# Linear attention with a router gate: the token blocks laid out as part, chunk, tile, token, each at its own offset modulo 128 B

## The chip, the cores and the metric

One core of one Trainium2 chip runs the whole program in one launch. The metric is the device time in microseconds (us) of one execution. TensorE is called PE here, VectorE DVE, ScalarE ACT, GpSimd POOL and SyncE SP; PEld is PE's row for weight loads. A program of one core has one time per execution, and the figure for a kernel is the median of its runs.

## The reference

The input is 2,048 tokens of 512 features, in 4 batches of 512. All is float32. Cut to what matters:

```
xn   = layernorm(x)                              # over the 512 features
qkv  = silu(xn @ w_qkv.T)                        # 16 heads of 128: q, k, v
out  = lightning attention(q, k, v)              # linear attention with a decay per head, a running 128x128 state
out  = norm_w * out / sqrt(mean(out^2) + 1e-6)   # over the 2,048 head features of a token
gate = sigmoid(xn @ w_gate.T)                    # 2,048 per token
s    = (gate * out) @ w_out.T                    # back to 512 features

p    = softmax(xn @ router_w.T + router_b)       # 64 experts
w    = top 8 of p, the rest 0
u    = xn * sum(w) + w @ expert_bias
x    = x + s * silu(u)
```

Four large products carry the work: those with the v, the q and k, the gate and the output weights.

## The kernel before, in words

**Products.** Each large product is done by a scheme of seven sub-products instead of eight (Strassen's, in Winograd's form). Tokens are split by batch into two halves, and features into two halves of 256. The token side gives seven blocks, `B11`, `T2`, `T3`, `T1`, `B21`, `T4`, `B22` (the list `PRODUCTS`); the `T` blocks are sums of `B` blocks. The weight side gives seven partners, `A11`, `S2` and so on.

**Two parts.** Every operand of these products is split into a high part, rounded to the type `fp32r`, and a low part, the rest (`split_hi` on ACT, L110; `split_lo` on DVE or POOL, L113). A sub-product is made of three passes: high by high, high by low, low by high (`PASSES`). With 256 features as two chunks of 128 (`KC = 2`), each of the seven sub-products takes 2 x 3 = 6 matmuls. `unit` (matmul at L516) runs seven sub-products with their sums; `plain_unit` (L546) runs eight without the scheme, for the first two tiles of tokens.

**The blocks.** The seven blocks of a pair of batches (`p` is 0 or 1) cover `NT = 4` tiles of 128 tokens. A block is one place in SBUF, made by `block`:

```
blocks[p, n] = xpool.tile([P, NT, 2, KC, P], F32R, tag=f"x{slot}", name=f"blk_{n}_{p}")
```

that is, per partition: tile, part, chunk, token, 2,048 values or 8 KB. `p = 0` uses four places of pool `xa` (tags `x0` to `x3`) and three of `xb` (`x4` to `x6`); `p = 1` uses three places of a later pool `xc` and then the four of `xa`.

**Stages.** There are three, one after the other, with some overlap.

1. *V units*, from the start to about 180 us. For 16 combinations of tile and group of weights, `v_unit` makes the v columns. The block is here the stationary operand, 128 tokens of one tile, part and chunk; the moving operand is 512 weight columns. Meanwhile the next tile is normalised, transposed on PE, summed (`token_sums`) and split into its blocks (`split_blocks`). The blocks of `p = 1` are made first in the same places, and stored to DRAM tile by tile (`keep_blocks`, 28 DMAs of SP, L319); those of `p = 0` are then made again from the stored transposes.
2. *Head units*, to about 851 us: for each pair of batches 24 units of two heads' gates, or one head's q and k (`gate_unit`, `qk_unit`). Here the weights, of 128 columns, are stationary, and the block moves, all four tiles of one part and chunk, 512 tokens:

```
return w.of[wn][:, wi, bass.ts(c, P)], blocks[p, xn][:, :, xi, c]
```

   Between sub-products the attention of the head before is run: matmuls `sa` (L672), `kt` (L675), `ss` (L695), `o` (L757, L759) in full fp32. At the change from `p = 0` to `p = 1` the blocks of `p = 1` are loaded from DRAM (`load_block`, L211, seven DMAs of 1 MB).
3. *Output product*, to the end. The matmul at L1228 has 256 moving columns: the split output weights `wr` move, and the split attention results `yr` are stationary. `split_wo` puts the weights of sub-products 1 and 2 into the places `x0` to `x3` of `xa`, which the blocks have left; the others lie in other pools.

**Order.** The schedule is written by hand: the lists `after[0]` to `after[6]` of a unit hold what is issued after each sub-product, and each engine runs its queue in program order. SP issues nearly all DMAs.

Of the kernel before, what the change touches and what calls it, by code (L numbers as in the profile page):

```python
# [1 line left out]

# [6 lines left out]
F32 = mybir.dt.float32  # L9
F32R = mybir.dt.float32r  # L10
# [4 lines left out]
P = 128  # L15
NH = 16
# [4 lines left out]
LN_EPS = 1e-05  # L21
RMS_EPS = 1e-06
WARM = 32

# [14 lines left out]
PRODUCTS = (  # L39
    ("A11", "B11", 0, True),  # L40
    ("S2", "T2", 1, True),
    ("S3", "T3", 2, True),
    ("S1", "T1", 3, True),
    ("A12", "B21", 0, False),
    ("A22", "T4", 2, False),
    ("S4", "B22", 3, False),
)
# [13 lines left out]
def kernel(  # L61
# [13 lines left out]
    nc = tc.nc  # L75
# [5 lines left out]
    NT = N // P  # L81
    KC = FC // 2
    VH = NH // 4
    VW = VH * P
# [3 lines left out]
    def pool(stack, name, bufs=1, **kw):  # L88
        return stack.enter_context(tc.tile_pool(name=name, bufs=bufs, **kw))


    def left(stack, name, bufs=1):
        return pool(stack, name, bufs, side="left", reuse_waits="tile")

    def right(stack, name, bufs=1):
        return pool(stack, name, bufs, side="right", reuse_waits="tile")

    const = pool(ctx, "const")
    wk = pool(ctx, "wk", 2)
    small = pool(ctx, "small", 4)  # L100
    dram = pool(ctx, "dram", space=DRAM)
# [7 lines left out]
    def split_hi(hi, src):  # L109
        nc.scalar.copy(hi, src)  # L110

    def split_lo(eng, lo, src, hi):
        eng.tensor_tensor(lo, src, hi.bitcast(F32), ALU.subtract)  # L113
# [7 lines left out]
    ones = const.tile([P, 1], F32, tag="ones", name="ones")  # L121
    mhalf = const.tile([P, NT], F32, tag="mhalf", name="mhalf")
    W = 2 * P
    decay_row = const.tile([NH, W], F32, tag="decay_row", name="decay_row")
    by_row = const.tile([P, 2], F32, tag="rest_of", name="rest_of")
    rest_of, slope_of = by_row[:, 0:1], by_row[0:NH, 1:2]
    kdecay = const.tile([P, NH], F32, tag="kdecay", name="kdecay")
# [12 lines left out]
    scores_d = [dram.tile([P, NT, E], F32, tag=f"sc{b}", name=f"scd_{b}") for b in range(B)]  # L140
    wT_d = [dram.tile([P, NT, P], F32, tag=f"wT{b}", name=f"wTd_{b}") for b in range(B)]
    blocks_d = {
        n: dram.tile([P, NT, 2, KC, P], F32, tag=f"b{n}", name=f"bd_{n}") for _, n, _, _ in PRODUCTS
    }


    NM, NQ, H2 = len(PRODUCTS), NG // 2, F // 2
# [13 lines left out]
    def warm_up(n):  # L161
        ps = ps_o.tile([P, P], F32, tag="o", name="warm")
        for _ in range(n):
            nc.tensor.transpose(ps, ident, ident)
# [34 lines left out]
    xb_stack = ExitStack()  # L199
    XN = [n for _, n, _, _ in PRODUCTS]  # L200
    NX = 4
    xa = pool(ctx, "xa")
    xb = left(xb_stack, "xb")
    blocks = {}

    def block(p, i, xpool, slot):
        n = XN[i]
        blocks[p, n] = xpool.tile([P, NT, 2, KC, P], F32R, tag=f"x{slot}", name=f"blk_{n}_{p}")

    def load_block(p, i):  # L210
        nc.sync.dma_start(out=blocks[p, XN[i]].bitcast(F32), in_=blocks_d[XN[i]])  # L211
# [47 lines left out]
    def transpose(stage, p, j, t, copy=True):  # L259
        b = p * PB + j  # L260
        if j == 0:
            xfs[p, t] = stage.tile([P, PB, FC, P], F32, tag="xf", name=f"xf_{p}_{t}", bufs=2)
        pt = ps_sc.tile([P, FC, P], F32, tag="sc", name=f"pt_{b}_{t}")
        for c in range(FC):
            nc.tensor.transpose(pt[:, c, :], xts[b, t][:, bass.ts(c, P)], ident)
        if copy:
            nc.scalar.copy(xfs[p, t][:, j], pt)
        return pt
# [3 lines left out]

    def split_blocks(p, t, eng, srcs):
        for n, src in srcs:
            blk = blocks[p, n][:, t]
            split_hi(blk[:, 0], src)
            split_lo(eng, blk[:, 1], src, blk[:, 0])


    def token_sums(eng, xf, s):  # L280
# [35 lines left out]

    def keep_blocks(p, t):
        for n in XN:
            nc.sync.dma_start(out=blocks_d[n][:, t], in_=blocks[p, n].bitcast(F32)[:, t])  # L319


    lg = {}
# [214 lines left out]
    def plain_unit(name, operands, sink, after):  # L537
        for i in range(2):
            ps = [ps_mm.tile([P, N], F32, tag="mm", name=f"d{i}{j}_{name}") for j in range(2)]
            for k in range(2):  # L540
                for j in range(2):
                    xn = (("B11", "T1"), ("B21", "B22"))[k][j]
                    for c in range(KC):
                        for n, (wi, xi) in enumerate(PASSES):
                            lhsT, rhs = operands(f"A{i + 1}{k + 1}", xn, wi, xi, c)
                            nc.tensor.matmul(  # L546
                                ps[j], lhsT, rhs, start=(k == 0 and c == 0 and n == 0),
                                stop=(k == 1 and c == KC - 1 and n == len(PASSES) - 1),
                            )
                    if k == 1:  # L550
                        sink(i, j, ps[j])
                for fs in (after[0:1], after[1:3], after[3:5], after[5:7])[2 * i + k]:
                    for f in fs:
                        f()
# [4 lines left out]
    def silu_of(dst, src, then=None):  # L559
        nc.scalar.activation(dst, src, AF.Silu)  # L560
        if then is not None:
            then()


    def v_weights(p, g, rawp, sump, wp):
        def loads(raw):
            r = raw.rearrange("p i k (c w) -> p i k c w", c=KC)
            per = VH // GH
            return [
                (r[:, i, k, :, bass.ts(j, GH * P)], w_v[(2 * g + i) * per + j][:, bass.ts(k, KC)])  # L570
                for i in range(2) for k in range(2) for j in range(per)
            ]
        return Weights(f"v_{p}_{g}", KC * VW, rawp, sump, wp, loads, True)

    def v_unit(p, g, t, w, outp, after, direct=False):
        name = f"v_{p}_{g}_{t}"

        def operands(wn, xn, wi, xi, c):
            return blocks[p, xn][:, t, xi, c], w.of[wn][:, wi, bass.ts(c, VW)]

        def sink(i, j):
            dst = outp.tile([P, VW], F32, tag="vout", name=f"vo{i}{j}_{name}")

            def store():
                nc.sync.dma_start(out=v_d[p * PB + j, 2 * g + i][t], in_=dst)
            return dst, lambda src: silu_of(dst, src, store)

        if direct:
            plain_unit(name, operands, lambda i, j, ps: sink(i, j)[1](ps), after)
            return  # L590
        unit(
            name, operands, lambda ps: sink(0, 0)[1](ps),
            [lambda: sink(1, 1), lambda: sink(0, 1), lambda: sink(1, 0)], after,
        )
# [11 lines left out]

    def head_operands(p, w):
        def operands(wn, xn, wi, xi, c):
            return w.of[wn][:, wi, bass.ts(c, P)], blocks[p, xn][:, :, xi, c]
        return operands  # L610


# [247 lines left out]
    def split_wo(m, j, w):  # L860
        pool_, tag = (
            (op, f"w{m}{j}") if m == 0 else (xa, f"x{2 * m - 2 + j}") if m < 3 else (late, f"w{min(m % 6, m)}{j}")
        )
        if m == 6:
            tag = f"w3{j}"
        wr = pool_.tile([P, 2, NQ, H2], F32R, tag=tag, name=f"wr_{m}_{j}", bufs=1)
        split_hi(wr[:, 0], w)
        for i in range(2):
            c = bass.ts(i, NQ // 2)
            split_lo(nc.vector if m else nc.gpsimd, wr[:, 1, c], w[:, c], wr[:, 0, c])  # L870
        wos[m, j] = wr
# [104 lines left out]
    stage = right(vs_stack, "stage", 4)  # L976
    rawp, sump = right(vs_stack, "vraw"), right(vs_stack, "vsum")
    vwp, vout = left(vw_stack, "vw", 8), left(vw_stack, "vout", 4)
    ws = [v_weights(0, g, rawp, sump, vwp) for g in range(NV)]
    tiles = [(p, t) for p in range(NP) for t in range(NT)]  # L980
    again = [(p, t) for p in reversed(range(NP)) for t in range(NT)]
# [17 lines left out]
    sig = small.tile([P, NT], F32, tag="var", name="table")  # L999
    warm_up(WARM)  # L1000
    for i, n in enumerate(XN):
        block(0, i, xa if i < NX else xb, i)
        blocks[1, n] = blocks[0, n]
# [8 lines left out]
    pt = [transpose(stage, 0, j, 0, False) for j in range(PB)]  # L1012
    nc.vector.tensor_copy(xfs[0, 0][:, 0], pt[0])
    b11, b12, b21, b22 = halves(xfs[0, 0])
    split_hi(blocks[0, "B11"][:, 0, 0], pt[0][:, 0:KC])
    ws[0].split_one("A11", nc.vector, hi=True)
    split_lo(nc.gpsimd, blocks[0, "B11"][:, 0, 1], b11, blocks[0, "B11"][:, 0, 0])
    nc.scalar.copy(xfs[0, 0][:, 1], pt[1])
    nc.sync.dma_start(out=xf_d[0], in_=xfs[0, 0])
    load_pair(stage, *tiles[2])  # L1020
# [11 lines left out]
    for k, (p, t) in enumerate(tiles + again):  # L1032
# [22 lines left out]
        if k < NP_FIRST:  # L1055
            for i in range(2 * k, 2 * k + 2):
                after[2 + 2 * (i % 2)].append(lambda i=i: ws[0].sum_of(i, nc.vector))
            for i, n in enumerate((("S1", "S2"), ("S3", "S4"))[k]):
                eng = nc.gpsimd if i else nc.vector
# [37 lines left out]


    attp = right(ha_stack, "att", 2)
    xc = None  # L1100
    xc_stack = ExitStack()

    steps = [(p, m, g) for p in range(NP) for m in range(NM) for g in range(NG)]
# [30 lines left out]
    for i, (p, kind, n, w) in enumerate(todo):  # L1134
# [102 lines left out]
    for i, (p, m, g) in enumerate(steps):  # L1237
# [111 lines left out]
```

## Time and profile before

| What | Value |
|---|---|
| Median of 3 runs | 1058.5 us (1058.11 to 1059.04) |
| The profiled execution | 1058.03 us |
| Its span, first to last instruction | 1056.2 us |
| Granted PE clock | 1.00 in every slice |
| PE busy, V stage (window 24 to 180 us) | 156.0 of 156.0 us |
| PE busy, head stage (180 to 520, 520 to 851) | 335.8 of 340.0, 331.0 of 331.0 us |
| PE busy, output stage (851 to 1056) | 198.8 of 205.0 us |
| POOL busy in the same four windows | 113.7, 257.0, 253.2, 54.6 us |
| Matmuls | 6,338 in the trace |

The profile page gives for each engine its busy time, and slices of the span in tenths. Matmuls are pipelined: the length of one holds its way through the array, and two neighbours overlap. What one matmul costs on a PE that never waits is therefore the gap from its start to the next one's start, which is worked out from the starts that the timeline view lists. A timeline line holds: start in us, length in us, engine, source line, operation, tiles (out<-in), shape and count. A row of the table of groups holds: line, engine, operation, tiles, shapes, count, then busy us and mean ns of one, then idle time before and what ended it.

### The profile page before, as it was taken

How to read it: one execution, taken by the hardware profiler on the slowest of the kernel's cores; microseconds unless marked ns; L12 is line 12 of the kernel's file. 1: busy time of each engine (PE TensorE's matmuls, PEld its weight loads, DVE VectorE, ACT ScalarE, POOL GpSimd, SP SyncE). 2: the span in 40 equal slices, each digit the busy share in tenths (PEclk: the TensorE clock that was granted, in tenths of full speed). 3: DMA queues.
4: the chain of work that ended last, by engine and by line, in shares of the span. 5: the costliest groups of instructions: out<-in, count | busy, mean ns of one | idle time of the engine just before them, and what ended most of it. 6: DMA issues, size and time to landing. Idle time of an engine off the chain costs nothing.

```text
span 1056.2 us, 17629 instructions
## 1 busy us (share of the span) xinstructions
PE 1043.6 (99%) x6338; PEld 924.6 (88%) x6338; DVE 640.3 (61%) x1017; ACT 552.0 (52%) x969; POOL 691.2 (65%) x698
## 2 busy tenths in 40 slices
PE   9999999999999999999999999999999999999997
PEld 7888888888888888888888888888888889999997
DVE  6666543356565787775554555545555558698667
ACT  5555555545545454455554555555545545574632
POOL 5888781857788687787777778877678743024013
PEclk9999999999999999999999999999999999999999
DMA  7556737523334376663863323533334236989863
GB/s 246 172 198 245 264 140 227 161 85 115 126 120 155 100 249 196 195 219 125 293 223 118 120 76 105 166 120 115 105 109 132 80 135 233 343 294 301 288 215 102
DMA packets 128838, 185.12 MB, mean 175 GB/s; under 512 B 11104, under 2 KB 72688, under 8 KB 127856
## 3 DMA queue, kind: packets, MB, share of 16 engines
q1 hardware_dynamic: 127856, 183.56, 52.0%
q8 instruction: 50, 0.82, 0.3%
q10 hardware_dynamic: 896, 0.44, 0.2%
q14 instruction: 36, 0.29, 0.1%
HBM read 115.26 MB, written 70.80 MB: 176 GB/s over the span
## 4 chain that ended last, share of the span: by engine, by line
PE 83%; DVE 8%; DMA 3%; ACT 2%; issue 2%; POOL 0%; SPq 0%; ACTq 0%; DVEq 0%
PE u_qk L516 26%; PE u_g L516 13%; PE u_v L516 13%; PE acc L1228 8%; PE sa L672 5%; PE o L757 5%; PE ss L695 4%; PE o L759 4%; DMA yin<-y 3%; PE d_v L546 2%; PE kt L675 2%; DVE yr L113 2%; PE lg L332 1%; DVE yS L720 1%; DVE wr L113 1%
## 5 line engine op out<-in xcount | busy, mean ns | idle before, releaser
L1228 PE MATMUL acc<-wr,yr 128*128 128x256 f32 x1344 | 163.7, 282 | 1.3 <-DVE a_o L900 1.3
L1228 PEld LDWEIGHTS acc<-wr,yr 128*128 128x128 f32 x1344 | 161.7, 190 | 3.3 <-DVE a_o L900 1.7
L516 PE MATMUL u_qk<-blk_T,ws_qk 128*128 128x512 f32 x576 | 141.7, 395 | 0.7 <-DVE k L507 0.7
L769 POOL TENSOR_TENSOR sqs<-sqs,sq 128x512 f32<-128x512 f32 x60 | 78.3, 1305 | 88.8 <-ACT sq L768 88.8
L516 PEld LDWEIGHTS u_qk<-blk_T,ws_qk 128*128 128x128 f32 x576 | 106.8, 188 | 23.8 <-issue 1.3
L113 POOL TENSOR_TENSOR ws_qk<-sum_qk,ws_qk 128x512 fp32r<-128x512 f32 x64 | 89.6, 1411 | 23.8 <-ACT ws_qk L110 23.5
L516 PE MATMUL u_qk<-blk_B,wa_qk 128*128 128x512 f32 x384 | 101.6, 400 | 0.0
L880 POOL TENSOR_TENSOR u<-u,x 128x256 f32<-128x256 f32 x28 | 32.4, 1179 | 101.0 <-DVE u L879 93.1
L113 DVE TENSOR_TENSOR yr<-yin,yr 128x1024 fp32r<-128x1024 f32 x56 | 75.5, 1352 | 35.6 <-ACT yr L110 35.5
L560 ACT ACTIVATE k<-k 128x512 f32<-128x512 f32 x64 | 40.4, 632 | 106.0 <-DVE k L507 106.0
L757 PE MATMUL o<-at,vin 128*128 128x128 f32 x512 | 88.4, 275 | 0.0
L516 PEld LDWEIGHTS u_qk<-blk_B,wa_qk 128*128 128x128 f32 x384 | 69.8, 189 | 13.7
L110 ACT CAST yr<-yin 128x1024 fp32r<-128x1024 f32 x56 | 58.3, 1045 | 43.7 <-PE acc L1228 37.2
L757 PEld LDWEIGHTS o<-at,vin 128*128 128x128 f32 x512 | 74.9, 192 | 2.5
L761 DVE SCALAR_TENSOR_TENSOR y<-o,nw,gt 128x512 f32<-128x512 f32 x64 | 47.7, 750 | 45.1 <-PE o L759 45.0
L681 ACT ACTIVATE kd<-kt,kdecay 128x384 f32<-128x384 f32 x64 | 37.2, 581 | 71.5 <-PE kt L675 71.5
L759 PE MATMUL o<-qd,st 128*128 128x128 f32 x384 | 74.3, 275 | 0.0
L516 PE MATMUL u_g<-blk_T,ws_g 128*128 128x512 f32 x288 | 72.5, 396 | 0.0
L768 ACT ACTIVATE sq<-o 128x512 f32<-128x512 f32 x60 | 35.8, 597 | 69.5 <-POOL sqs L769 43.2
L683 POOL TENSOR_TENSOR qd<-q,dec 128x384 f32<-128x384 f32 x64 | 71.2, 1134 | 0.0
L672 PE MATMUL sa<-q,k 128*128 128x128 f32 x512 | 67.9, 276 | 1.5 <-ACT q L560 1.4
L672 PEld LDWEIGHTS sa<-q,k 128*128 128x128 f32 x512 | 64.3, 191 | 5.3 <-ACT q L560 2.7
(199 smaller groups left out, 2387.1 us busy)
## 6 DMA issues: line engine op xcount, KB each, us to landing
yin<-y SPq DMA_DIRECT2D x56, 512.0 KB, 4.9
v<-vo_v SPq DMA_DIRECT2D x64, 256.0 KB, 2.7
raw_qk<-in_w_head_dram SPq DMA_DIRECT2D x64, 256.0 KB, 3.9
vin<-v SPq DMA_DIRECT2D x64, 256.0 KB, 3.4
y<-yS SPq DMA_DIRECT2D x64, 256.0 KB, 2.1
y<-y SPq DMA_DIRECT2D x48, 256.0 KB, 2.1
woin<-wo SPq DMA_DIRECT2D x18, 512.0 KB, 5.5
x<-in_x_dram SPq DMA_DIRECT2D x32, 256.0 KB, 4.6
```

The costliest lines, as they stand in the source:

```text
L110: nc.scalar.copy(hi, src)
L113: eng.tensor_tensor(lo, src, hi.bitcast(F32), ALU.subtract)
L516: nc.tensor.matmul(ps, lhsT, rhs, start=(first and c == 0 and n == 0), stop=(c == KC - 1 and n == len(PASSES) - 1), skip_group_check=not f ...
L560: nc.scalar.activation(dst, src, AF.Silu)
L672: nc.tensor.matmul(pa[:, c], k[:, c], q[:, c], start=True, stop=True)
L683: nc.gpsimd.tensor_tensor(qd[s], q[:, 1:], d[:, 1, None, :].to_broadcast([P, NT - 1, P]), ALU.mult)
L695: nc.tensor.matmul(ps[:, c], kd[s][:, c], v_of(b, h, c), start=True, stop=True)
L757: nc.tensor.matmul(o, v_of(b, h, c), at[s][:, c], start=True, stop=(c == 0))
L759: nc.tensor.matmul(o, st[s][:, c - 1], qd[s][:, c - 1], start=False, stop=True)
L761: nc.vector.scalar_tensor_tensor(y, po, nw[:, h : h + 1], gts[s], ALU.mult, ALU.mult)
L769: nc.gpsimd.tensor_tensor(sq[b], sq[b], s1, ALU.add)
L1228: nc.tensor.matmul(acc[t // 2][:, t % 2], yr[:, yi, bass.ts(t, P)], wos[m, g // NQ][:, wi, g % NQ], start=(first and g == 0 and n == 0 and ...
```

## The change

The values of a block are ordered by part, chunk, tile, token instead of tile, part, chunk, token. In the head units the 512 moving values become one run of 2 KB; before, they are four runs of 512 B with starts 2 KB apart. In the V units the 128 stationary values are one run of 512 B before and after. A split into a block writes two runs of 128 values, 2 KB apart; before, one run of 256. The DRAM copy of a block has the new order too, so the 28 stores move four runs of 512 B per partition; before, one of 2 KB. The loads move 8 KB runs as before.

Each place of a block is made 32 values (128 B) longer, and the block starts in it at an offset that its place is given in `SHIFTS`. The function `shifted` does this, and `split_wo` uses it too where it takes a place in `xa`. The decay row, 1 KB per partition, moves from the constants to the first stage's pool, which makes room for the longer places. Nothing is added to or taken from any engine's instructions, and their order is kept.

In the built programs the blocks start modulo 128 B at these places, in the order of `PRODUCTS`:

| | B11 | T2 | T3 | T1 | B21 | T4 | B22 |
|---|---|---|---|---|---|---|---|
| p = 0 before | 32 | 32 | 32 | 32 | 32 | 32 | 32 |
| p = 0 after | 0 | 16 | 48 | 64 | 80 | 96 | 112 |
| p = 1 before | 96 | 96 | 96 | 32 | 32 | 32 | 32 |
| p = 1 after | 112 | 0 | 48 | 0 | 16 | 48 | 64 |

The V units' moving weights start at 32, the head units' stationary weights at 96, before and after.

```diff
+SHIFTS = {
+    (False, "x0"): 96, (False, "x1"): 112, (False, "x2"): 16, (False, "x3"): 32,
+    (False, "x4"): 48, (False, "x5"): 64, (False, "x6"): 80,
+    (True, "x0"): 16, (True, "x1"): 32, (True, "x2"): 80,
+}
...
-    decay_row = const.tile([NH, W], F32, tag="decay_row", name="decay_row")
...
-        n: dram.tile([P, NT, 2, KC, P], F32, tag=f"b{n}", name=f"bd_{n}") for _, n, _, _ in PRODUCTS
+        n: dram.tile([P, 2, KC, NT, P], F32, tag=f"b{n}", name=f"bd_{n}") for _, n, _, _ in PRODUCTS
...
+    def shifted(pool_, tag, name, shape, **kw):
+        by = SHIFTS[pool_ is xc, tag] // 4
+        n = math.prod(shape)
+        t = pool_.tile([P, n + 32], F32R, tag=tag, name=name, **kw)[:, by : by + n]
+        a, b, c = shape[0], shape[1], shape[2]
+        return t.rearrange("p (a b c) -> p a b c", a=a, b=b)
+
     def block(p, i, xpool, slot):
         n = XN[i]
-        blocks[p, n] = xpool.tile([P, NT, 2, KC, P], F32R, tag=f"x{slot}", name=f"blk_{n}_{p}")
+        t = shifted(xpool, f"x{slot}", f"blk_{n}_{p}", (2, KC, NT * P))
+        blocks[p, n] = t.rearrange("p i c (t m) -> p i c t m", m=P)
...
-            blk = blocks[p, n][:, t]
-            split_hi(blk[:, 0], src)
-            split_lo(eng, blk[:, 1], src, blk[:, 0])
+            hi, lo = (blocks[p, n][:, i, :, t] for i in range(2))
+            split_hi(hi, src)
+            split_lo(eng, lo, src, hi)
...
-            nc.sync.dma_start(out=blocks_d[n][:, t], in_=blocks[p, n].bitcast(F32)[:, t])
+            nc.sync.dma_start(out=blocks_d[n][:, :, :, t], in_=blocks[p, n].bitcast(F32)[:, :, :, t])
...
-            return blocks[p, xn][:, t, xi, c], w.of[wn][:, wi, bass.ts(c, VW)]
+            return blocks[p, xn][:, xi, c, t], w.of[wn][:, wi, bass.ts(c, VW)]
...
-            return w.of[wn][:, wi, bass.ts(c, P)], blocks[p, xn][:, :, xi, c]
+            return w.of[wn][:, wi, bass.ts(c, P)], blocks[p, xn][:, xi, c].rearrange("p t m -> p (t m)")
...
-        wr = pool_.tile([P, 2, NQ, H2], F32R, tag=tag, name=f"wr_{m}_{j}", bufs=1)
+        if pool_ is xa:
+            wr = shifted(xa, tag, f"wr_{m}_{j}", (2, NQ, H2))
+        else:
+            wr = pool_.tile([P, 2, NQ, H2], F32R, tag=tag, name=f"wr_{m}_{j}", bufs=1)
...
+    decay_row = stage.tile([NH, W], F32, tag="decay_row", name="decay_row", bufs=1)
```

More of the change, by code (lines that the diff above doesn't have):

```diff
@@ L1 @@
+import math
 from contextlib import ExitStack
@@ L201 @@
     NX = 4
+    xc = None
     xa = pool(ctx, "xa")
@@ L1014 @@
     b11, b12, b21, b22 = halves(xfs[0, 0])
-    split_hi(blocks[0, "B11"][:, 0, 0], pt[0][:, 0:KC])
+    split_hi(blocks[0, "B11"][:, 0, :, 0], pt[0][:, 0:KC])
     ws[0].split_one("A11", nc.vector, hi=True)
-    split_lo(nc.gpsimd, blocks[0, "B11"][:, 0, 1], b11, blocks[0, "B11"][:, 0, 0])
+    split_lo(nc.gpsimd, blocks[0, "B11"][:, 1, :, 0], b11, blocks[0, "B11"][:, 0, :, 0])
     nc.scalar.copy(xfs[0, 0][:, 1], pt[1])
@@ L1099 @@
     attp = right(ha_stack, "att", 2)
-    xc = None
     xc_stack = ExitStack()
```

## The prediction, before the result

> **What bounds the kernel now.** I read the page first: busy times, slices, the chain. These are whole lines of it.
>
> ```profile
> span 1056.2 us, 17629 instructions
> PE 1043.6 (99%) x6338; PEld 924.6 (88%) x6338; DVE 640.3 (61%) x1017; ACT 552.0 (52%) x969; POOL 691.2 (65%) x698
> PEclk9999999999999999999999999999999999999999
> PE 83%; DVE 8%; DMA 3%; ACT 2%; issue 2%; POOL 0%; SPq 0%; ACTq 0%; DVEq 0%
> ```
>
> TensorE works all the time at the full granted clock, and no other engine is busy for more than 65%. So the time is the sum of the gaps from one matmul's start to the next, and this change alters no wait and no order: compared instruction by instruction, the two built programs have the same instructions in the same order on every engine with the same semaphore values; only addresses and access patterns differ. I need gaps, and the timeline of PE gives them: the starts of two groups, divided by the matmuls between them (a group's own length also holds the last matmul's latency).
>
> First the V units, where a block is the weight and the moving operand is 512 values in one run:
>
> ```profile
> 120.60 4.24 PE L516 MATMUL u_v<-w_S_v,blk_T 128*128 128x512 f32 x18
> 124.68 1.52 PE L516 MATMUL u_v<-w_A_v,blk_B 128*128 128x512 f32 x6
> 126.04 1.52 PE L516 MATMUL u_v<-w_A_v,blk_T 128*128 128x512 f32 x6
> ```
>
> (124.68 - 120.60)/18 = 226.7 ns. Then the head units, where the block moves, in four runs of 128 values, 2 KB apart:
>
> ```profile
> 478.68 1.63 PE L516 MATMUL u_qk<-blk_B,wa_qk 128*128 128x512 f32 x6
> 480.15 1.54 PE L516 MATMUL u_qk<-blk_T,wb_qk 128*128 128x512 f32 x6
> 481.53 1.54 PE L516 MATMUL u_qk<-blk_B,ws_qk 128*128 128x512 f32 x6
> 482.90 0.60 PE L757 MATMUL o<-at,vin 128*128 128x128 f32 x4
> ```
>
> (481.53 - 480.15)/6 = 230.0 and (482.90 - 481.53)/6 = 228.3. Over all 1,814 head gaps under 250 ns in the trace the mean is 229.6 ns. (The first group, 245 ns each, holds one gap of 315 ns: the first matmul after full-fp32 work pays some 88 ns more, 105 times; the change does not touch that.)
>
> Last the output product, 256 columns. These are four short windows of its timeline, each of 26 matmuls:
>
> ```profile
> 901.43 3.11 PE L1228 MATMUL acc<-wr,yr 128*128 128x256 f32 x26
> ...
> 907.02 3.28 PE L1228 MATMUL acc<-wr,yr 128*128 128x256 f32 x26
> ...
> 1021.30 3.28 PE L1228 MATMUL acc<-wr,yr 128*128 128x256 f32 x26
> ...
> 1024.17 3.23 PE L1228 MATMUL acc<-wr,yr 128*128 128x256 f32 x26
> ```
>
> Less the last one's 0.28 us, over 25 gaps: 113.2, 120.0, 120.0 and 118.0 ns. The work is the same; what differs, by the addresses in the built program, is where `wr` (moving) and `yr` (weight) start modulo 128 B. In the second and third both start at the same place (32 and 32; 96 and 96), in the first and fourth 64 B apart. Over the whole stage: 119.7 ns (591 gaps, same place) against 116.8 ns (686 gaps, 64 apart; these sit near 113 or near 118 for stretches).
>
> So a column costs (226.7 - 120.0)/256 = 0.417 ns, and a remainder stands on every matmul whatever its length: 13.3 ns where both operands start alike, 11.3 or 6.6 ns when they are 64 B apart. For 512 strided columns it is 229.6 - 213.3 = 16.3 ns. The next matmul's weight load starts 3 ns after a matmul does, so both read SBUF together; I take the remainder for the cost of that meeting.
>
> **The change, part by part.**
>
> *One run instead of four.* 2,016 head matmuls (the L516 groups with `blk` moving). At the V units' gap each saves 229.6 - 226.7 = 2.9 ns: 5.8 us.
>
> *Starts modulo 128 B.* By the built program, V weights go from 32 (where the moving weights also stand, all 684) to 0, 16, 48, 64, 80, 96, 112; head blocks, against weights at 96, to the same seven in the first half and 112, 0, 48, 0, 16, 48, 64 in the second, so that 144 start alike instead of 432; of the output product 264 matmuls stop starting alike. The trace holds only 0 and 64 B of distance. From below: no saving. From above: the best row, 6.7 ns off the remainder. I take the mean of the 64 B rows, 119.7 - 116.8 = 2.9 ns, nearest because most matmuls will have some distance and none can be read directly: V 684 x 2.9 = 2.0 us; heads, beyond the first step, (2,016 - 144) x 2.9 = 5.4 us; output 264 x 2.9 = 0.8 us.
>
> A rule speaks against both steps. The Trainium skill, "SBUF — State Buffer", section "Who interferes with whom", gives PE two independent read ports, one for the moving operand and one for weight loads, and states: "PE and ACT never wait on anyone." By it the sum would be nothing and the time 1058; this trace's 113 against 120 ns for equal work disagrees.
>
> *Splits into a block* (78 on ACT, 150 on POOL, 6 on DVE) now write two runs of 128 values instead of one of 256. The nearest rows, writes of two runs (`wa`) and one (`ws`) of equal size:
>
> ```profile
> L110 ACT CAST ws_g<-sum_g 128x512 fp32r<-128x512 f32 x32 | 19.4, 607 | 0.0
> L110 ACT CAST wa_g<-raw_g 128x512 fp32r<-128x512 f32 x16 | 9.8, 611 | 0.0
> L113 POOL TENSOR_TENSOR ws_g<-sum_g,ws_g 128x512 fp32r<-128x512 f32 x32 | 42.0, 1314 | 33.0 <-ACT ws_g L110 33.0
> L113 POOL TENSOR_TENSOR wa_g<-raw_g,wa_g 128x512 fp32r<-128x512 f32 x16 | 20.8, 1302 | 0.4 <-ACT wa_g L110 0.4
> ```
>
> +4 ns and -12 ns: nothing. They belong to the V stage, where PE is busy 156.0 of 156.0 us (the window 24 to 180) while POOL works 113.7 and ACT 82.9: covered; uncovered, 78 x 4 ns = 0.3 us.
>
> *Keeping blocks:* 28 stores of 256 KB go from one 2 KB run per partition to four of 512 B. The nearest row is `vin`, loaded in runs of 512 B:
>
> ```profile
> vin<-v SPq DMA_DIRECT2D x64, 256.0 KB, 3.4
> bd_T<-blk_T SPq DMA_DIRECT2D x16, 256.0 KB, 3.3
> ```
>
> Issue takes 0.46 us there (median) against 0.46 to 0.63 here. SP issues them in four bursts between 77 and 117 us, some 4 us each, with idle gaps of about 3 us before the next V store; the blocks are read back from 490 us on. Zero; if a piece cost double, a burst would use 4 us more and V stores queued behind it would come 1 us late, covered by the four `vout` buffers. The seven loads back keep their 8 KB runs and only land at odd multiples of 16 B; the third product reads its block (issued by 517.6, landing at most 13.2 us later) at about 533.9: 3 us of cover. The decay row's new place costs nothing: it is written ahead of the first V matmul and stored once.
>
> *Sum:* 5.8 + 2.0 + 5.4 + 0.8 = 14.0 us of PE. Nearly all of it reaches the end: in the head stage POOL, next, is busy 253 of 331 us (window 520 to 851). I take off 5% for stretches that the chain gives to DVE and DMA: 13.3 us. The profiled execution took 1058.03 us (1.8 outside its span), 0.5 under the median: 1058.5 - 13.3 = 1045.2, say **1045 us**.
>
> **The rivals.**
>
> *Only the stride counts* for 512 columns. The head halves by start speak for it: blocks at 96, like the weights, had 230.4 ns, the others 229.5, a difference of 0.9 only. Then 5.8 + 0.8 = 6.6, with 5% off 6.3: 1052.
>
> *The remainder falls to its best row, 6.6 ns.* Two stretches of the output stage show 113 ns throughout. Heads 2,016 x (16.3 - 6.6) = 19.6, V 684 x 6.7 = 4.6, output 264 x 6.5 = 1.7, sum 25.9, with 5% off 24.6: 1034. Against it: most 64 B rows stayed at 118.
>
> *Nothing moves:* 1058. For it, contiguous matmuls that are as slow as strided ones, in the first V tiles:
>
> ```profile
> 19.20 1.54 PE L546 MATMUL d_v<-w_A_v,blk_T 128*128 128x512 f32 x6
> 20.59 2.88 PE L546 MATMUL d_v<-w_A_v,blk_B 128*128 128x512 f32 x12
> ```
>
> (20.59 - 19.20)/6 = 231.7 ns. So one run alone does not ensure 226.7.
>
> *Slower: starts at odd multiples of 16 B.* Every start in this trace is a multiple of 32. If a read unit is 32 B or more, an odd start adds a unit to each read, or meets the weight load worse. By the new addresses this touches 1,152 head, 384 V and 192 output matmuls. Priced at one more remainder, 1,728 x 13.3 ns = 23.0, less the 13.3 gained: 9.7 slower, 1068. It decides from 13.3/1,728 = 7.7 ns each. Nothing in the trace shows such a cost, and nothing excludes it.
>
> **How the numbers follow.** Forecast 0.45, stride alone 0.17, best row 0.16, nothing 0.10, odd starts 0.12. A difference under 0.2% (2.1 us) cannot be told from none here. The first three are faster: 0.78; same 0.10; slower 0.12. The range runs from the best row (1034) over the forecast and stride alone to no change (1059): it leaves out the odd starts and half of the best row's case.
>
> **What would show it.** Right: the same 18 V matmuls under 4.08 us; six head matmuls clear of fp32 work in about 1.34 us instead of 1.38; PE still 99% busy; ACT and POOL rows of `blk` unchanged. Wrong: head groups still at 1.37 to 1.38 (stride and start do not matter), or gaps that split by odd and even multiples of 16 B; or a PE wait on `blk` loads near 530 us.

## The result, and the profile after

The changed kernel takes 1065.9 us (median of 4 runs, 1064.9 to 1068.4) against 1058.7 (4 runs, 1058.1 to 1059.0): a ratio of 1.0071, 95% interval 1.0059 to 1.0083. It is 7.2 us slower where 13.3 us less were forecast. The profiled execution took 1065.44 us. These are its page's span, busy times, granted clock and chain of waits:

```profile
span 1063.7 us, 17629 instructions
...
PE 1051.7 (99%) x6338; PEld 925.2 (87%) x6338; DVE 638.4 (60%) x1017; ACT 552.2 (52%) x969; POOL 691.4 (65%) x698
...
PEclk9999999999999999999999999999999999999999
...
PE 87%; DVE 6%; DMA 2%; ACT 2%; issue 1%; POOL 1%; SPq 0%; DVEq 0%; ACTq 0%; POOLq 0%
```

The span grew by 7.5 us and PE's busy time by 8.1; the clock is full, the other engines' times are the same to 2 us, and the chain has more PE, not more waiting. PE's timeline shows where. First the V units (`unit` is now at L530; columns: start, length, group):

```profile
120.09 1.56 PE L530 MATMUL u_v<-w_A_v,blk_B 128*128 128x512 f32 x6
121.48 4.35 PE L530 MATMUL u_v<-w_S_v,blk_T 128*128 128x512 f32 x18
125.68 1.55 PE L530 MATMUL u_v<-w_A_v,blk_B 128*128 128x512 f32 x6
127.06 1.55 PE L530 MATMUL u_v<-w_A_v,blk_T 128*128 128x512 f32 x6
128.45 0.86 PE L530 MATMUL u_v<-w_S_v,blk_B 128*128 128x512 f32 x3
```

(125.68 - 121.48)/18 = 233.3 ns where the kernel before had 226.7. Then the head units, where the block now moves in one run:

```profile
484.59 1.55 PE L530 MATMUL u_qk<-blk_T,wb_qk 128*128 128x512 f32 x6
485.98 1.55 PE L530 MATMUL u_qk<-blk_B,ws_qk 128*128 128x512 f32 x6
487.37 0.61 PE L771 MATMUL o<-at,vin 128*128 128x128 f32 x4
```

Both groups have (485.98 - 484.59)/6 = 231.7 ns. Over the whole trace (start-to-start gaps of consecutive matmuls, those under 250 ns) the means went like this:

| gaps | before | after | matmuls | product |
|---|---|---|---|---|
| V, with the 96 of `plain_unit` | 227.4 | 232.3 | 684 | +3.4 us |
| heads | 229.6 | 232.2 | 2,016 | +5.1 us |
| output, 256 columns | 118.1 | 118.1 | 1,344 | 0 |

All gaps between 200 and 250 ns add up to 602.2 us before (2,630 gaps) and 610.4 after (2,631): +8.2. Longer gaps, the waits among them, came to 51.8 and 50.9 us. So the loss is this one class of gaps, and no new wait stands behind it. The stores that the change cuts into four are there but cost nothing. The packets of the page, and from the DMA view the stores of `T` blocks (count, KB each, median us from issue to landing):

```profile
DMA packets 139590, 185.12 MB, mean 174 GB/s; under 512 B 11104, under 2 KB 87024, under 8 KB 138608
```

```profile
bd_T<-blk_T SPq DMA_DIRECT2D x16, 256.0 KB, 3.3
```

That is 10,752 packets more than before's 128,838 (28 stores x 128 partitions x 3), and still 3.3 us a store.

### The profile page after: what moved, and what is told of

Read it like the earlier page. It is cut to its first block, busy times and chain, and to the rows that moved or that the text cites. A ratio compares the mean times of both kernels' runs of the same rounds, so it can differ in the third digit from the quotient of the medians.

```text
span 1063.7 us, 17629 instructions
## 1 busy us (share of the span) xinstructions
PE 1051.7 (99%) x6338; PEld 925.2 (87%) x6338; DVE 638.4 (60%) x1017; ACT 552.2 (52%) x969; POOL 691.4 (65%) x698
## 4 chain that ended last, share of the span: by engine, by line
PE 87%; DVE 6%; DMA 2%; ACT 2%; issue 1%; POOL 1%; SPq 0%; DVEq 0%; ACTq 0%; POOLq 0%
PE u_qk L530 26%; PE u_v L530 13%; PE u_g L530 12%; PE acc L1245 12%; PE sa L686 5%; PE o L771 5%; PE ss L709 4%; PE o L773 3%; PE d_v L560 2%; DMA yin<-y 2%; PE kt L689 2%; PE lg L346 1%; DVE yS L734 1%; DVE wosum L760 1%; PE pt L279 1%
## 5 line engine op out<-in xcount | busy, mean ns | idle before, releaser
L530 PE MATMUL u_qk<-blk_T,ws_qk 128*128 128x512 f32 x576 | 143.6, 398 | 1.0 <-DVE k L521 1.0
L530 PEld LDWEIGHTS u_qk<-blk_T,ws_qk 128*128 128x128 f32 x576 | 106.9, 188 | 25.8 <-issue 1.8
L530 PE MATMUL u_qk<-blk_B,wa_qk 128*128 128x512 f32 x384 | 102.4, 402 | 0.0
L530 PEld LDWEIGHTS u_qk<-blk_B,wa_qk 128*128 128x128 f32 x384 | 69.9, 189 | 14.1
L530 PE MATMUL u_g<-blk_T,ws_g 128*128 128x512 f32 x288 | 73.3, 399 | 0.0
```

What stands on the lines that cost most here:

```text
L530: nc.tensor.matmul(ps, lhsT, rhs, start=(first and c == 0 and n == 0), stop=(c == KC - 1 and n == len(PASSES) - 1), skip_group_check=not f ...
```

## The experiments

Every V, head, output and chain matmul of these runs is fp32r with a weight load of its own. For each of them I took from the built program the start of the weight operand less the start of the moving operand, in SBUF bytes per partition; this is called the distance. In all kernels but the three chains PE's instructions, their order and their semaphores are those of the kernel before; only addresses and access patterns differ, and in e5 to e8, where more room is taken, a few waits on POOL and SP fall otherwise (one load of `yin` in e5, e7 and e8 waits for a later matmul; e8, whose head weights share one place, has 29 wait instructions fewer on POOL and one fewer on SP). Each ratio is against runs of the kernel before taken beside it (medians of 1058.4 to 1059.7 us); V and heads are means of the gaps under 250 ns in the profiled execution, in ns. In the diffs, `...` stands for lines left out.

| run | what differs from before | us | ratio, 95% | V | heads |
|---|---|---|---|---|---|
| after | new order, places +128 B, offsets | 1065.9 | 1.0071 (1.0059 to 1.0083) | 232.3 | 232.2 |
| e1 | new order, places +128 B | 1064.5 | 1.0055 (1.0040 to 1.0070) | 231.5 | 230.8 |
| e2 | old order, places +128 B, offsets | 1068.0 | 1.0084 (1.0064 to 1.0105) | 232.3 | 232.1 |
| e3 | new order, places +128 B, all alike modulo 128 | 1065.1 | 1.0064 (1.0045 to 1.0083) | 231.6 | 231.1 |
| e4 | new order | 1059.0 | 0.9998 (0.9986 to 1.0011) | 227.2 | 229.6 |
| e6 | new order, places +256 B | 1058.5 | 0.9995 (0.9984 to 1.0005) | 227.3 | 229.6 |
| e7 | heads at a distance of 96 | 1066.8 | 1.0058 (1.0038 to 1.0079) | 227.4 | 234.1 |
| e5 | V and most heads at 240 | 1061.3 | 1.0024 (1.0011 to 1.0036) | 228.3 | 231.1 |
| e8 | heads at 192, odd starts | 1055.7 | 0.9965 (0.9953 to 0.9978) | 228.4 | 226.9 |

**The new order in longer places, no offsets (e1).**

```diff
-SHIFTS = {(False, "x0"): 96, (False, "x1"): 112, ...}
+SHIFTS = {(c, f"x{i}"): 0 for c in (False, True) for i in range(7)}
```

> The change's order of values (part, chunk, tile, token) and its longer places, but every offset 0: all blocks start where they started before (32 modulo 128 B; the first three of the second half at 96). Undisturbed gaps before: V 227.1 ns, heads 229.6; after the change: V 232.3, heads 232.2. Theory 'mixed starts cost' (the offsets cost 5 ns a V matmul and the stride saves): V back at 227, heads 227 to 228, time about 1058.7 - 2,016 x 2.5 ns = 1053 to 1055 us. Rival 'the order costs' (parts now lie 4 KB apart, chunks 2 KB): V stays at 232, heads at 232, about 1066 us.

1064.5 us: without any offset most of the loss is there. PE's timeline shows two kinds of V group side by side:

```profile
119.88 1.53 PE L526 MATMUL u_v<-w_A_v,blk_T 128*128 128x512 f32 x6
121.25 1.56 PE L526 MATMUL u_v<-w_S_v,blk_B 128*128 128x512 f32 x6
122.64 1.56 PE L526 MATMUL u_v<-w_A_v,blk_B 128*128 128x512 f32 x6
```

228.3 ns for the first (121.25 - 119.88, by 6), 231.7 for the second. By block, T1, T2 and T4 have 228.9 to 230.5 and B11, B21, B22 and T3 have 232.6 to 233.1. All are at the same start modulo 128; modulo 256 the first three are at a distance of 0 and the others at 128, since places of 8,320 B put every other block 128 B on. The first three do not come down to 226.7, probably because their matmuls stand six at a time between groups at 128 and do not settle (see the last section).

**The offsets with the old order (e2).**

```diff
-        t = shifted(xpool, f"x{slot}", f"blk_{n}_{p}", (2, KC, NT * P))
+        t = shifted(xpool, f"x{slot}", f"blk_{n}_{p}", (NT, 2, KC * P))
...
```

> The change's offsets and longer places with the old order of values (tile, part, chunk, token): heads read four runs again, stores are 2 KB runs. Theory 'mixed starts cost': V at 232, heads at 232 or more (stride and mixed starts together, up to 229.6 + 5 = 235), time 1064 to 1070 us. Rival 'the order costs': V at 227 and heads at 229.6, time 1058.7.

1068.0 us and the gaps of the changed kernel in V (232.3) and heads (232.1), although the head matmuls again read four runs of 128. Two head groups of PE's timeline:

```profile
487.58 1.55 PE L530 MATMUL u_qk<-blk_T,wb_qk 128*128 128x512 f32 x6
488.97 1.31 PE L530 MATMUL u_qk<-blk_B,ws_qk 128*128 128x512 f32 x5
```

1.39 us by 6 is 231.7 ns, as after. The order of the values plays no part in the loss.

**All starts alike modulo 128 (e3).**

```diff
-SHIFTS = {(False, "x0"): 96, (False, "x1"): 112, ...}
+SHIFTS = {(c, f"x{i}"): 0 if c else 64 for c in (False, True) for i in range(7)}
...
+    vwp.tile([P, 16], F32, tag="pad", name="pad", bufs=1)
```

> The change's order, and all operands of the 512-wide matmuls start alike: blocks, V weights and head weights all at 96 modulo 128 B; output weights as before the change. Theory 'mixed starts cost, like starts are the cheap state': V 226.7 ns, heads 226.7, time 1058.7 - 2,016 x 2.9 ns = 1053 us or somewhat less. Rival 'the order costs': V and heads near 232, 1066 us. Rival of the forecast 'like starts are the dear state' (13.3 ns against 6.6 to 11): heads no better than in the run with the order alone.

1065.1 us, V 231.6. Three V groups of PE's timeline:

```profile
126.14 1.56 PE L526 MATMUL u_v<-w_A_v,blk_B 128*128 128x512 f32 x6
127.53 1.53 PE L526 MATMUL u_v<-w_A_v,blk_T 128*128 128x512 f32 x6
128.90 0.40 PE L526 MATMUL u_v<-w_S_v,blk_B 128*128 128x512 f32 x1
```

231.7 ns for the first (1.39 by 6), 228.3 for the second. So it is not that alike starts are dear and different ones cheap, nor the reverse, as long as starts are taken modulo 128. Taken modulo 256 the V matmuls have 229.8 ns at a distance of 0 and 232.8 at 128.

**The gaps alone (m1).** Chains of 36 matmuls on operands in place, eight full-fp32 transposes between chains. The moving start is 128 modulo 256, the weight start goes from 0 on in steps of 16 B, so the distance goes from 128 to 240.

```diff
+    for d in range(8):
+        run([(wt(4 * d + 1024 * (k % 3 == 2)), one(2048 * (k % 3 == 1))) for k in range(N)])
+    ... the same with one weight throughout, with four(...) for one(...), with 256 columns
```

> Only chains of matmuls on random data, no part of the reference is computed; groups of 36, set apart by eight full-fp32 transposes. Groups: A one weight and one run of 512 columns, weight start 0 to 7 steps of 16 B further than the moving one; B the same in three passes with two parts each; C as B in four runs 2 KB apart; D as A with 256 columns; E both operands 16, 32, 64 B further; F and G with a start that goes on by 16 B every six matmuls, of the moving operand and of the weight; H in the V units' order of passes with parts 1 KB or 4 KB apart. Theory 'mixed starts cost': A and B have one gap near 226.7 ns at step 0 and others above it, F and G above the mean of B's steps; C about 3 ns over B. Theory 'odd multiples of 16 B cost': the odd steps of A and B lie 5 ns or more above the even ones, and E's 16 B above its 32 and 64 B. Theory 'the order costs': H with 4 KB lies 5 ns above H with 1 KB.

From 128 to 240, means after the sixth gap: 232.7, 233.3, 233.2, 230.0, 228.9, 231.8, 233.4, 226.7 ns. Four strided runs gave 232.7, 233.3, 233.2, 230.0, 228.9, 231.8, 233.4, 226.7: the stride costs nothing. The chains at 144, with one run and with four:

```profile
94.73 8.64 PE L48 MATMUL acc<-mov,wts 128*128 128x512 f32 x36
...
168.34 8.64 PE L48 MATMUL acc<-mov,wts 128*128 128x512 f32 x36
```

One weight for all three passes gave the same to 0.6 ns, and so did parts 4 KB apart instead of 1 KB. A weight start that goes on by 16 B every six matmuls gave 230.6 and 231.4, near the mean of the eight, 231.2: mixing starts costs nothing by itself. The same chain once more gave 233.4 at 128 and 233.8 at 160, so a pair of starts does not always have one value.

**Sixteen distances (m2).** The same over the full 256 B, from a moving start of 0 modulo 256, and four of them again with the weight 256 and 512 B further.

```diff
+    for d in range(16):
+        run([(wt(4 * d + 1024 * (k % 3 == 2)), one(BASE + 2048 * (k % 3 == 1))) for k in range(N)])
+    for far in (64, 128):
+        ... the same with wt(far + 4 * d + ...) for d in (0, 4, 8, 12)
```

> No part of the reference is computed: chains of fp32r matmuls alone, all with operands in place, on the pattern of three passes. Per chain one distance, weight start less moving start, in steps of 16 B from 0 to 240 B, the moving start a fixed multiple of 256 B plus 128. Theory (the gap goes by the distance modulo 256 B): 512 columns give 226.7 ns at 0 and at 16 or 240 B, about 229 at 192, 232 to 235 at all others, with 128 at 232.5 although it is 0 modulo 128; 256 or 512 B further the gaps of 0, 64, 128 and 192 repeat within 0.3 ns. In chains of 12 straight after full-fp32 transposes the gaps at distance 0 start above 226.7 and come down to it within about ten matmuls. Rival (modulo 128 B, as the prediction had it): 128 B gives what 0 gives, and 16 steps show the same eight values twice. Rival (only the absolute start counts): the gaps show no order in the distance, and chains that are 256 B further differ.

PE's timeline, whole chains at distances of 0, 64, 128, 192 and 240 (a chain's length holds 34 gaps after its first, so 0.21 us is 6 ns a gap):

```profile
11.90 8.47 PE L49 MATMUL acc<-mov,wts 128*128 128x512 f32 x36 [1.42 <-ACT wts L32]
...
48.81 8.64 PE L49 MATMUL acc<-mov,wts 128*128 128x512 f32 x36
...
85.89 8.61 PE L49 MATMUL acc<-mov,wts 128*128 128x512 f32 x36
...
122.85 8.49 PE L49 MATMUL acc<-mov,wts 128*128 128x512 f32 x36
...
150.52 8.44 PE L49 MATMUL acc<-mov,wts 128*128 128x512 f32 x36
```

Settled means: 226.8 at 0, 226.7 at 240, 228.8 at 192, 230.0 at 176, and 231.9 to 234.4 at the other twelve; 128 has 232.4, not what 0 has. 256 B further, 0, 64, 128 and 192 have 226.7, 233.2, 232.4 and 228.9; 512 B further 226.7, 233.4, 233.5 and 228.9. So the distance counts modulo 256, with one value 1.1 ns off (128, 512 B further; the run before had both 232.7 and 233.4 there). Of the two neighbours of 0 only 240 is cheap; 16 has 233.3. With 256 columns the range is 116.7 (208) to 120.0 (0, 112 and 144), so another order: 0 is among the dearest there.

**The new order alone (e4)**, in places of 8 KB and with every offset 0:

```diff
...
-        t = pool_.tile([P, n + 32], F32R, tag=tag, name=name, **kw)[:, by : by + n]
+        t = pool_.tile([P, n], F32R, tag=tag, name=name, **kw)[:, by : by + n]
...
```

> The kernel before with the new order of values in a block alone (part, chunk, tile, token): places 8 KB as before, no offsets, so every operand starts where it did before modulo 256 B. Theory (distance modulo 256 B, stride free): V gaps 227 ns, head gaps 229.6, time 1058.5, within 0.2% of before: one run instead of four saves nothing. The prediction's term (one run instead of four saves 2.9 ns on 2,016 matmuls): head gaps 226.7 and 1052 to 1053. Rival (the new order itself is what costs, by its stores in four pieces or its new start of each tile): about 1064, as with the new order in longer places.

0.9998: no change. The head groups of PE's timeline, which now read one run:

```profile
481.14 1.54 PE L527 MATMUL u_qk<-blk_T,wb_qk 128*128 128x512 f32 x6
482.51 1.54 PE L527 MATMUL u_qk<-blk_B,ws_qk 128*128 128x512 f32 x6
483.88 0.49 PE L768 MATMUL o<-at,vin 128*128 128x128 f32 x3
```

1.37 us by 6 is 228.3 ns, as before with four runs, and the mean of all is 229.6 again.

**Places 256 B longer (e6)**, every offset 0:

```diff
...
-        t = pool_.tile([P, n + 32], F32R, tag=tag, name=name, **kw)[:, by : by + n]
+        longer = 0 if pool_ is xc else 64
+        t = pool_.tile([P, n + longer], F32R, tag=tag, name=name, **kw)[:, by : by + n]
```

> The changed kernel's order of values, no offsets, and its places 256 B longer instead of 128 (those of the pool for the second pair are not longer). Against the run with the order alone in places 128 B longer, only that length differs; every operand of the V and the head units then starts where it did before, modulo 256 B. Theory (distance modulo 256 B): V gaps 227 ns, head gaps 229.6, 1058.5 us, within 0.2% of before. Rival (longer places or the new order in them cost by themselves, through DMAs or addresses that are not 8 KB apart): V 231.5, heads 230.8, 1064.5.

Two V groups and a head group (the last line ends it) of PE's timeline:

```profile
120.47 4.24 PE L527 MATMUL u_v<-w_S_v,blk_T 128*128 128x512 f32 x18
124.55 1.52 PE L527 MATMUL u_v<-w_A_v,blk_B 128*128 128x512 f32 x6
...
481.73 1.54 PE L527 MATMUL u_qk<-blk_B,ws_qk 128*128 128x512 f32 x6
483.10 0.60 PE L768 MATMUL o<-at,vin 128*128 128x128 f32 x4
```

V has 4.08 us by 18, 226.7 ns, and the heads 1.37 by 6, 228.3, as before. 0.9995: the loss of e1 is gone, by 128 B more in the length of a place. Longer places cost nothing; their length modulo 256 does.

**Heads at a dear distance, blocks untouched (e7).** Pads in the pool of head weights and in the one of the second pair's first three blocks:

```diff
+            hpools["w"].tile([P, 40], F32R, tag="pad", name="pad_h", bufs=1)
+                xc.tile([P, 16], F32R, tag="pad", name="pad_xc")
...
```

> The kernel before with its own order; only the head weights and the three places of the second pair are moved by pads, so that all 2,016 head matmuls have weight start less moving start = 96 modulo 256 B (before: 1,584 at 192, 432 at 0). The V units stay at 0. Theory: head gaps 234.3 ns as in the chains alone, V gaps 227 as before; 2,016 x 4.7 = 9.5 us more matmul time, of which 80 to 100% reach the end: 1066 to 1068. Rival (the slowdown of the changed kernel is in the blocks, their order, offsets or DMAs, not in the distance): 1058.5, since no block of the first pair moves. Rival (modulo 128 B): 96 is dear, 64 cheap, the two cannot be told apart here.

Heads 234.1 ns, V 227.4, 1066.8 us. PE's timeline of the head groups:

```profile
485.27 1.56 PE L518 MATMUL u_qk<-blk_T,wb_qk 128*128 128x512 f32 x6
486.67 1.57 PE L518 MATMUL u_qk<-blk_B,ws_qk 128*128 128x512 f32 x6
488.08 0.61 PE L759 MATMUL o<-at,vin 128*128 128x128 f32 x4
```

(488.08 - 486.67)/6 = 235.0. The blocks of the first pair, their order, their stores and loads are those of the kernel before, so the cost is in the pair of starts. 2,016 x 4.5 = 9.1 us of PE, of which 6.1 (0.58%, interval 0.38 to 0.79) show in the time.

**V and heads at 240 (e5).**

```diff
+        by, longer = (0, 0) if xpool is xc else (4, 64)
+    vwp.tile([P, 8], F32R, tag="pad", name="pad_v", bufs=1)
+                padded.append(wp.tile([P, 48], F32R, tag="pad", name="pad_h", bufs=1))
...
```

> An attempt at a faster version: the order of before, the seven places of the first pair 256 B longer with each block 16 B in, and two pads, so that V (684) and 1,584 of the 2,016 head matmuls have a distance of 240 modulo 256 B; the other 432 heads stay at 0, the output product keeps its distances but for 96 matmuls that go from 192 to 0 (+3 ns each, 0.3 us). Theory: V gaps 227 as before; the 1,584 head gaps fall from 229.2 to between 226.9 and 228.5 (chains of 12 behind full-fp32 work had 226.9 and 228.7 in the chains alone): 1 to 3.5 us less, 1055 to 1058, so 0.1 to 0.3% faster. Rival (16 B of offset cost something, as odd multiples of 16 B were suspected to): V and head gaps at 233 and 1066 or more. Rival (blocks between full-fp32 work never settle): head gaps stay at 229 and the time at 1058.5.

A miss: 1061.3 us, 0.24% slower. Two head groups at 240:

```profile
482.56 1.56 PE L521 MATMUL u_qk<-blk_T,wb_qk 128*128 128x512 f32 x6
483.95 1.55 PE L521 MATMUL u_qk<-blk_B,ws_qk 128*128 128x512 f32 x6
485.34 0.60 PE L762 MATMUL o<-at,vin 128*128 128x128 f32 x4
```

1.39 us by 6 is 231.7 ns. Over the trace V has 228.3 (moving start 64), the heads at 240 have 231.6 (moving start 48), not 226.7. The distance is not the whole rule.

**The same distances at other starts (m3).**

```diff
+    for d in (0, 64, 192, 240):
+        for start in (0, 16, 32, 48, 64, 80, 112, 128):
+            chain(start, d, N)
```

> No part of the reference is computed: chains of fp32r matmuls alone, as in the run over sixteen distances, but the distances 0, 64, 192 and 240 B each at eight moving starts (0, 16, 32, 48, 64, 80, 112, 128 B modulo 256). Asked because V units at 240 with the moving operand at 64 had 228.3 ns in the attempt at a faster version, head units at 240 with it at 48 had 231.5, and the chains with it at 0 had 226.7. Theory that the distance alone counts: 226.7, 233.3, 229 and 226.7 ns at every start. Theory that the start counts too: 240 keeps 226.7 at start 0 and goes to 228 at 64 and to about 231.5 at 48, while 0 and 192 at start 32 give 226.7 and 229 as in the kernel before. Theory that it is the kernel around the units (short chains after full-fp32 work, other engines' traffic): all starts alike in chains of 36, and only the chains of 12 lie higher at 240.

| distance | starts 0, 32, 64, 128 | starts 16, 48, 80, 112 |
|---|---|---|
| 0 | 226.7 to 227.4 | 230.1, 233.3, 230.1, 230.1 |
| 64 | 233.2 to 233.4 | 226.7, 229.0, 229.0, 229.0 |
| 192 | 228.8 to 228.9 | 226.7 |
| 240 | 226.7, 228.3, 228.3, 228.3 | 231.6 to 231.8 |

(Means after the sixth gap, in ns.) Whether the moving start is an even or an odd multiple of 16 B counts, in either direction. The two values of the run before, 228.3 at start 64 and 231.6 at 48, come out to 0.1 ns. Within the parities some single starts differ (48 at a distance of 0, 16 at 64, 0 at 240). PE's timeline at a distance of 192, starts 0, 16 and 32, with one group of the eight full-fp32 transposes that stand between chains:

```profile
158.51 8.50 PE L49 MATMUL acc<-mov,wts 128*128 128x512 f32 x36
166.85 1.04 PE L38 MATMUL apart<-ident 128*128 128x128 f32 x8
167.64 8.42 PE L49 MATMUL acc<-mov,wts 128*128 128x512 f32 x36
...
176.69 8.49 PE L49 MATMUL acc<-mov,wts 128*128 128x512 f32 x36
```

The settled gaps are no noise about a mean: they repeat in a fixed cycle, 226, 227, 227 at the best pairs, 226, 229, 232 at 192 and even starts, 227, 234, 235, 230 at 240 and odd ones. Chains of 12 at start 32 and distance 240 after transposes went into one cycle in two of four cases (226, 227, 227) and into another in the other two, so one pair of starts can have more than one cycle.

**A version built from that table (e8).** Heads keep 192 but start at odd multiples of 16 B (moving 48, weight 240); V goes to 240.

```diff
+        by, longer = (4, 48 if slot == 2 else 64) if xpool is xc else (4, 64)
-            wa = wp.tile([P, 2, 2, w], F32R, tag="wa", name=f"wa_{n}")
+            all_ = wp.tile([P, 14 * w + 64], F32R, tag="w", name=f"wh_{n}")[:, 4 : 4 + 14 * w]
+            wa = all_[:, 0 : 4 * w].rearrange("p (i j c) -> p i j c", i=2, j=2)
+            ... wb and ws likewise, from 4 * w and from 6 * w
...
```

> A version built from the chains: all 2,016 head matmuls keep the distance of 192 B modulo 256 that most of them have before, but both operands start at odd multiples of 16 B (moving 48, weight 240), where the chains alone had 226.7 ns against 228.8 at even starts, settled within four matmuls. The V units go to a distance of 240 with the moving operand at 64 (chains and the attempt before: 228.3 ns against 227.3). Order of values, blocks' shape and the output product's distances as before; the three head weights share one place and the places are longer, the constants of the router and the decay row lie elsewhere. Theory (the gap is set by the pair of starts modulo 256 B): head gaps 227 to 227.5 instead of 229.6, so 2,016 x 2.1 to 2.6 = 4.2 to 5.2 us less, V 684 x 1.0 = 0.7 us more; 3.5 to 4.5 us faster than the kernel before, a ratio of 0.9957 to 0.9967. Rival (odd multiples of 16 B cost, or other traffic sets the gaps in the whole kernel): head gaps 230 to 232 and a ratio of 1.001 to 1.005.

1055.7 us, 0.9965 (0.9953 to 0.9978): faster than both kernels. Its page and PE's timeline, a V group and two head groups:

```profile
span 1054.4 us, 17599 instructions
...
PE 1040.3 (99%) x6338; PEld 925.2 (88%) x6338; DVE 645.6 (61%) x1017; ACT 552.2 (52%) x969; POOL 691.3 (66%) x698
```

```profile
122.89 4.27 PE L519 MATMUL u_v<-w_S_v,blk_T 128*128 128x512 f32 x18
127.00 1.53 PE L519 MATMUL u_v<-w_A_v,blk_B 128*128 128x512 f32 x6
...
482.21 1.52 PE L519 MATMUL u_qk<-blk_T,wh_qk 128*128 128x512 f32 x6
483.57 1.52 PE L519 MATMUL u_qk<-blk_B,wh_qk 128*128 128x512 f32 x6
484.93 0.61 PE L760 MATMUL o<-at,vin 128*128 128x128 f32 x4
```

Heads 1.36 us by 6, 226.7 ns; V 4.11 by 18, 228.3. Heads gain 2,016 x 2.7 = 5.5 us, V loses 684 x 1.0 = 0.7: 4.8 of PE, and 0.35%, 3.7 us, in the time. V at an even start and distance 0 beside these heads should give the 0.7 back; it wasn't tried, as it needs blocks at two starts.

## Why the prediction was wrong

**What bounds the kernel: right.** PE is busy 99% at full clock, the time is the sum of its gaps, and the change acts through them alone. The working broke where it said what sets a gap, in the two steps that make up the whole saving of 14.0 us: the count of runs, and starts taken modulo 128 B.

**"One run instead of four", 5.8 us: nothing.** The step took V's 226.7 ns (one run) and the heads' 229.6 (four runs) and put the difference down to the runs. But the two also differ in distance: V is at 0 modulo 256, 1,584 of the heads at 192, where chains of one run and chains of four both have 228.9. The other 432 heads are at 0 like V and still have 230.4, with four runs (before) and with one (order alone): they stand close behind full-fp32 work, where the second to tenth gap lie between 226 and 236 by place, and only from the eleventh on have 226.6 to 226.9. With the order alone all heads stay at 229.6. The rows compared differed in two things, and the step priced the one that the change removes.

**"Starts modulo 128 B", 8.2 us less: 8.5 us more.** The evidence was output gaps at the same start and 64 B apart, 119.7 and 116.8 ns. By address those 64 B are 64 and 192 modulo 256, and the result was carried from 256 columns to 512, where the order is another: distance 0 is among the dearest with 256 columns (120.0) and is the cheapest with 512 beside 240 (226.8 and 226.7 from a moving start of 0); 64 is 117.8 and 233.2. So there is no remainder that stands on a matmul whatever its length. The V units left one of the best pairs there are, and their blocks went to distances of 32, 64, 112, 144, 176, 208 and 224, each at what the sixteen chains give for it, within 1.5 ns: 232.8, 232.7, 232.8, 232.6, 230.4, 231.8 and 233.0 ns in the trace. The modulus was wrong as well: places 128 B longer alternate by 128 modulo 256, which alone makes 0.55% of the loss of 0.71%.

**Splits, stores, loads: zero, right.** The splits into `blk_T` took 404 and 844 ns on ACT and POOL, against 403 and 846. The loads back took 9.3 and 11.8 us instead of 8.7 and 10.9, and no wait of PE came of it. The count of splits was misread, without effect on the sum: the program has 75 low splits on POOL and 3 on DVE, half of what is stated.

**The 5% taken off** looks too little: of 8.5 us of PE after, 7.5 came through to the span of the profiled execution, and in the time 6.1 of 9.1 with the heads at 96 and 3.7 of 4.8 with the last version. The intervals (6.2 to 8.8, 4.0 to 8.4 and 2.3 to 5.0 us) rule 5% out only for the heads at 96, where it would leave 8.6.

**The rivals.** "Only the stride counts" and "the remainder falls" fall with the two steps. "Nothing moves" had its row, `d_v` at 231.7 ns, read as one run that is slow; its gaps are those of a chain at distance 0 that has not settled behind full-fp32 work (after the first 228, 234, 236, 224, 230, 237, 228, 233, 230, then 226 or 227; the row covers the last four of these and the first two settled ones). "Slower, by odd multiples of 16 B" had the right side and the wrong mechanism, and that its 1068 lies near 1065.9 is chance, a sum of two wrong terms: V blocks at odd multiples have 231.8 ns, at even ones 232.8. The dear 13.3 ns per odd start do not exist; in the chains an odd start costs up to 6.5 or saves up to 6.7 ns, by the distance.

**A page weighed.** The Trainium skill, "SBUF — State Buffer", section "Who interferes with whom", gives PE two independent read ports and states: "PE and ACT never wait on anyone." Equal fp32r matmuls with a weight load each, whose gaps go from 226.7 to 234.4 ns by where their two operands start, do not fit two reads that never meet; that they meet at the ports was not shown. "TensorE: Matmul & The Clock Gate", section "Wait — 56ns, not 53.3ns?", gives N / 2.4 GHz + 2.5 ns, 215.7 for 512 columns; no settled mean at 512 columns here came under 226.7.

**Open.** Which part of the chip makes the cycles was not shown: that weight load and moving read meet is an argument, since the distance between them counts. The table holds for these shapes and passes. It does not settle the output product: at a distance of 192 with the moving start at 32, stretches of 22 to 48 gaps in the kernel before have means from 113.3 to 118.0 ns, so why the prediction's first window had 113 stays open.

## What to carry to other kernels

When all matmuls are back to back, look at the addresses before pricing a layout: take the weight start less the moving start modulo 256 B and the parity of the moving start in units of 16 B, measure the pairs in a chain of the same columns and type, and keep the length of a place a multiple of 256 B so that neighbours stay alike. Do not carry a start's price from one column count to another. And two rows that differ in more than one thing price neither: the stride was charged with what the start cost.

## What was not expected of the hardware

- The gap of a 512-column fp32r matmul with its weight load is 226.7 to 234.4 ns by the starts of the two operands modulo 256 B; that of 256 columns 116.7 to 120.0 in the chains, in another order, and down to 113.3 in a stretch of the output product.
- Most chains settle into a fixed cycle of a few values (two at a distance of 0 from a start of 16, 228 and 232; seven at 128), and after full-fp32 work this takes up to ten matmuls: at a distance of 192 with odd starts one to four, at 0 with even starts one to ten. Head units, which such work mostly cuts after 12 or 18 matmuls, therefore had 231.7 ns in their first block at distance 0, where long chains have 226.7.
- The first matmul after full-fp32 work has a gap of 311 to 322 ns whatever its operands' starts (512 columns, all chains but the first of a run). The full-fp32 matmul ahead of it has 28 to 31 ns (chains and the kernel before) instead of some 109: the eight transposes shown above take 0.79 us, seven times 109 and once 28. The change from one kind to the other so costs about 10 ns at most, not the 88 that the prediction reads from the first gap alone.
- Four runs of 128 values, 2 KB apart, move as fast as one run of 512.
